# A two-layer state-space network on one core: carried states copied by VectorE, one state's B no longer spread on the scan's path, dt's bias inside its product, the first convolution shared by four engines

## The chip, the cores and the metric

The kernel runs on one core of a Trainium2 chip. A core has TensorE (PE in the profile), VectorE (DVE), ScalarE (ACT), GpSimd (POOL) and SyncE (SP, which here only issues transfers). The metric is the device time of the whole program in microseconds.

## The reference

Eight images of 48 x 48 pixels with 192 channels go through two layers. Each layer is `x + layer(group_norm(x))`.

Layer 0 is a 2D selective scan. It projects to 384 inner channels and a gate, convolves 3 x 3 by channel, and runs the scan in four directions (rows, columns, and both backwards) with 16 states per channel:

```
x_dbl = einsum('bkdl,kcd->bkcl', xs, x_proj_w)     # 12 rows for dt, 16 for B, 16 for C
dt = softplus(einsum('bkrl,kdr->bkdl', dts, dt_w) + dt_bias)
h = exp(dt * A) * h + (dt * u) * B                 # per position, channel and state
y = sum over states of h * C
ys = ys + D * xs
```

The four directions are summed, normalised over channels, gated with `silu(z)` and projected back to 192 channels.

Layer 1 runs two passes (along columns of the image, then along rows), each a sum of a forward and a backward scan over lines of 48 positions, with a convolution of three taps, the same scan with its own weights, a gate and a projection.

## The kernel before

Channels lie on the 128 partitions, three groups (`NJ`) for the 384 channels. A chunk is 8 lines of 48 positions (`T` = 384), six chunks (`NC`) to an image. An **item** is one chunk of one direction of one image: 192 items in layer 0, 192 in layer 1. An item has 48 **segments**, one for each state and channel group (`NSEG` = 16 x 3).

For one segment:

- ACT makes the decay `exp(dt * A)` (`decays`, L435).
- The input of the scan, `dt * u * B`, is made in three ways. For most states, ACT or POOL **weighs** the transposed product `dtu` by B (`weighs`, L464 on ACT in three instructions per state, L459 on POOL in one), and PE transposes it back into PSUM (`places`, L512). For the **diagonal** states (4 and 11 in layer 0) ACT or POOL makes a diagonal matrix of B (`matrices`, L483 and L480), and PE multiplies `dtu` by it (L503). For the **direct** state (8 in both layers) PE spreads B over the partitions, and DVE multiplies that by `du` ahead of the scan (`scans`, L523).
- DVE runs the scan along 384 positions (L1059 in layer 0, L1298 in layer 1).
- After the three segments of a state, POOL multiplies the three results by C in place (`gathers`, L548), and PE transposes and sums them over the states into `y` (`adds`, L565). Four `h` buffers are in flight.

In layer 0 a direction's scan runs on from chunk to chunk, so the last state of an item is kept in `carry` and is the first value of the next item's scan. `put_carry` copies the last column of `h` (three values per partition) before the product with C; it is on POOL (L1030), at 16 copies for each of 160 items.

Each pair of items is prepared by `project`: PE multiplies `u` by `x_proj` (`xd_ps`, L295), an evacuation puts the 44 rows into `xd`, SP sends the C rows to memory so that they can be fetched spread over the partitions (`cc`), PE makes dt from the first 12 rows (`dt_ps`, L344), and ACT or DVE evacuates it with the bias (`biased`, L229 and L231). A softplus follows on ACT, then `products`: POOL makes `du = dt * u` (L372), PE transposes it, and ACT or DVE copies it to `dtu`.

The order of everything is made by a planner (`Plan`). Each piece of work is a `Need` with a due time counted in segments, a cost for each engine that could do it, and what must be done before it. The planner gives each to the engine that could start it first, and of several ready ones it takes the one due first. So a changed cost or due time moves instructions between engines and along their queues. `late` puts off the due time of a piece for one engine.

The rest of layer 0 is laid between the segments: `prologues` (projection and convolution of the next image, on PE by diagonal matrices, L767), `enters` (projections of items and their table loads), `tails` (norm, gate and projection of a finished chunk, run in the last six items of each image). The first image has no scan to hide behind; `first` does its projection and convolution. There PE convolves channel group 0 and four chunks of group 2, and DVE the rest (`by_vector`, L839 and L841).

Of the kernel before, what the change touches and what calls it, by code (L numbers as in the profile page):

```python
# [35 lines left out]

DIRECT = ((8,), (8,))

# [144 lines left out]
class Common:  # L183


    def __init__(self, ctx, tc):
# [23 lines left out]
        )  # L210

    def tables(self):

        self.nc.scalar.preload_act_table_set("natural_log_exp_and_others")
# [61 lines left out]
    def project(self, plan, pool, p, pair, lo, mid, hi):  # L276

        nc, mark = self.nc, plan.mark
        tiles = {}
        dts, evacs = [], []
        for i, item in enumerate(pair):
            g, wts = 2 * p + i, item["wts"]
            turned = item.get("turned")
            across = (lambda v: v.rearrange("p (h w) -> p h w", w=RT)) if turned else rows
            at = pace(mid if i else lo, hi if i else mid, 12)
            for j in range(NJ):  # L290
                n = Need(at(), {PE: item["cost"][0]}, item["ready"] if j == 0 else (), bank=(j == 0))
                yield n
                if j == 0:
                    ps, k = self.bank(n, "xd_ps"), n.bank
                nc.tensor.matmul(  # L295
                    across(ps[:E, :T]), wts["xp"][:, j, :], item["u"](j),
                    start=(j == 0), stop=(j == NJ - 1),
                )
            xd = pool.tile([E, T], F32, tag="xd", name="xd", bufs=1)
            got = Need(at(), COPY, [n] + self.xd_used, frees=k)  # L300
            yield got
            if turned:
                self.copy(
                    got.e, xd.rearrange("p (w h) -> p w h", h=S),
                    ps[:E, :T].rearrange("p (h w) -> p w h", w=RT),
                )
            else:
                self.copy(got.e, xd, ps[:E, :T])

            def send(e, i=i, xd=xd):  # L310
                if i == 0:
                    tiles["bc"] = self.bcd.tile([2, N, T], F32, tag="bc", name="bc")
                nc.sync.dma_start(tiles["bc"][i], xd[R + N : E, :])
                pair[i]["bc"] = tiles["bc"][i]

            after = [got] + ([mark("cc", g - 5, N // 2 - 1)] if g >= 6 else [])
            sent = Need(at(), {SP: 0.1}, after, lag=DMA, sets=[mark("bc", g)])
            yield sent
            send(SP)
            n = Need(at(), {PE: 0.3}, [got], bank=True)  # L320
            yield n
            ps, k = self.bank(n, "bt_ps"), n.bank
            for b in range(TB):
                nc.tensor.transpose(
                    ps[:, b * E : (b + 1) * E], xd[:, b * P : (b + 1) * P], self.ident[:E, :E]
                )
            after = [n] + ([mark("place", (g - 2 - i) * NSEG - 1)] if g >= 4 else [])
            n = Need(at(), {ACT: 0.16, DVE: 0.19}, after, frees=k, sets=[mark("bt", g)])
            yield n
            if i == 0:  # L330
                bt = pool.tile([P, 2, TB, E], F32, tag="bt", name="bt", bufs=2)
            item["bt"] = bt[:, i]
            self.copy(n.e, bt[:, i].rearrange("p b e -> p (b e)"), ps[:, : TB * E])
            for j in range(NJ):
                after = [got]
                if j == 0 and g >= 3:
                    after.append(mark("exp", (g - 2) * NSEG - 1))
                n = Need(at(), {PE: 0.83}, after, bank=True)
                yield n
                ps = self.bank(n, "dt_ps")  # L340
                if j == 0:
                    dt = pool.tile([P, NJ, T], F32, tag="dt", name="dt", bufs=3)
                    dts.append(dt)
                nc.tensor.matmul(  # L344
                    ps[:, :T], wts["dtw"][:, j * P : (j + 1) * P], xd[:R, :], start=True, stop=True
                )
                evacs.append(plan.then(
                    Need(at(), BIAS, [n], frees=n.bank),
                    lambda e, dt=dt, j=j, ps=ps, wts=wts: self.biased(
                        e, dt[:, j, :], ps[:, :T], wts["dtb"][:, j : j + 1]  # L350
                    ),
                ))
            self.xd_used = [n, sent]
        for item, dt in zip(pair, dts):
            item["dt"] = dt
        return evacs
# [4 lines left out]

    def products(self, plan, pool, items, others, diagonal):

        nc, mark = self.nc, plan.mark
        last = max(n for n in range(N) if n not in others)
        for g, item in enumerate(items):
            after = [mark("dt", g)] + ([mark("multiplied", g - 2), mark("turned", g - 2)] if g >= 2 else [])
            n = Need(g * NSEG - 20 - item.get("sooner", 0), {POOL: item["cost"][1]}, after, sets=[mark("du", g)])
# [32 lines left out]
    def stream(self, plan, pool, items, direct, diagonal, decay, scan, finish, held, kept, weighed):  # L401
# [66 lines left out]
        def matrices():  # L468
            for i, item in enumerate(items):
                for n in sorted(diagonal):  # L470
                    after = [mark("bt", i)]
                    if placed:
                        after += [mark("place", placed[-1] + j) for j in range(NJ)]
                    need = Need(i * NSEG + NJ * n - 6, {POOL: 0.8, ACT: 0.72}, after, sets=[mark("matrix", i, n)])
                    yield need
# [59 lines left out]
        def gathers():  # L535

            for f in range(total // NJ):
# [3 lines left out]
                if "carry" in item:  # L541
                    need = Need(NJ * f + 2.5, {POOL: 0.15}, after, sets=[mark("carry", i, n)])
                    yield need
                    item["carry"](need.e, n, hs[f])
# [60 lines left out]
        for lane in (fetches, decays, weighs, matrices, places, scans, gathers, adds):  # L605
            plan.start(lane())
        plan.start(self.products(plan, pool, items, (*direct, *diagonal), diagonal))


@with_exitstack  # L610
def layer0(ctx, cm, x, xs, x2, w, norm):
# [12 lines left out]

    cw, cb, xp, dtw, dtb = [load(n) for n in ("conv_w", "conv_b", "xp", "dtw", "dtb")]
    A, D, lnw, lnb, wout = [load(n) for n in ("A", "D", "ln_w", "ln_b", "out")]
# [18 lines left out]
    per = 4 * NC  # L645
    span = per * NSEG

    def piece(b, c, due, tag="xc", bufs=2, after=(), of=x):
# [156 lines left out]
    def first():  # L805
# [22 lines left out]
        def by_vector():  # L828

            for c in range(NC):  # L830
                for j in (1, 2) if c < 2 else (1,):
                    to = rows(u[:, j, c * T : (c + 1) * T])
                    for t in range(9):
# [6 lines left out]
                        else:  # L840
                            nc.vector.scalar_tensor_tensor(to, of, cw[:, j, t : t + 1], to, ALU.mult, ALU.add)  # L841

        plan.start(by_vector())

        def by_tensor(j, chunks, made):
# [13 lines left out]
        n = yield from by_tensor(0, range(2, NC), made)  # L859
        made = yield from matrices(2, -60, [n])  # L860
        n = yield from by_tensor(2, range(2, NC), made)
        yield Need(0, {SP: 0.1}, [mark("conv", j, c) for j in range(NJ) for c in range(NC)], sets=[mark("free")])
# [4 lines left out]
    def enters():  # L867
# [5 lines left out]
        for p in range(last + 1):  # L873
# [3 lines left out]
            if q < 3 and p < last:  # L877
                lo, mid, hi = g * NSEG - 56, g * NSEG - 46, g * NSEG - 30
                if q == 0 and b:
                    n = Need(lo - 10, {SP: 0.3}, [mark("du", g - 1), mark("v", b)], lag=9.0)  # L880
# [146 lines left out]
    def put_carry(e, q, h, rev):  # L1027
        to, of = carry[:, q * NJ : (q + 1) * NJ], h[:, :, 0 if rev else T - 1]
        if e == POOL:
            nc.gpsimd.tensor_copy(to, of)  # L1030
        else:
            nc.scalar.copy(to, of)

    items = []
    for b in range(NIMG):
        for k in range(4):
            rev = k >= 2
            order = range(NC - 1, -1, -1) if rev else range(NC)
            for n, c in enumerate(order):
                item = dict(  # L1040
                    b=b, k=k, c=c, reverse=rev, carried=(n > 0), A=A[:, k],
                    wts=dict(xp=xp[:, k], dtw=dtw[:, k, :], dtb=dtb[:, k, :]),
                    u=lambda j, k=k, c=c: by_rows(seen(u, j, k, c), k), turned=k % 2,
# [46 lines left out]
def layer1(ctx, cm, x2, xw, dst, w, norm):  # L1090
# [25 lines left out]

    cb, cw, dtb, A, D, wout = [load(n) for n in ("conv_b", "conv_w", "dtb", "A", "D", "out")]
    cm.negative_exp(A)
# [133 lines left out]
    def begins():  # L1252


        for p in range(pairs):
# [8 lines left out]
            for d in range(2):  # L1264
                i = 2 * p + d
                items[i].update(
                    D=D[:, 2 * stage + d], A=A[:, 2 * stage + d], ready=[mark("silu", i)] + loaded,
                    wts=dict(xp=xp[:, d], dtw=dtw[:, d], dtb=dtb[:, 2 * stage + d]),
                )
# [104 lines left out]
def laid_out(a):  # L1374
# [7 lines left out]
    def model(v):  # L1382

        v = v.reshape(*v.shape[:-2], NM, CP, v.shape[-1])
        return np.moveaxis(v, -2, 0)

    t = {}
    t["x"] = a["x"].reshape(NIMG, L, NM, CP).transpose(0, 3, 2, 1)
# [6 lines left out]
    t["w0_xp"] = np.moveaxis(inner(g("x_proj_w")), 2, 3)  # L1395
    t["w0_dtw"] = g("dt_w").transpose(2, 0, 1)
    t["w0_dtb"] = inner(g("dt_bias"))
    t["w0_A"] = np.moveaxis(inner(g("A_logs").reshape(4, DI, N).transpose(0, 2, 1)), 2, 3)
# [8 lines left out]
    t["w1_xp"] = np.moveaxis(inner(g("x_proj_w")), 2, 3)  # L1407
    t["w1_dtw"] = g("dt_proj_w").transpose(2, 0, 1)
    t["w1_dtb"] = inner(g("dt_proj_b"))
    t["w1_A"] = np.moveaxis(inner(g("A_log").transpose(0, 2, 1)), 2, 3)  # L1410
# [24 lines left out]
```

## Time and profile before

| | |
|---|---|
| median of 3 runs | 21024.0 us (21023.82 to 21025.34) |
| profiled execution | 21021.07 us, its span 21019.3 us |
| PE busy | 20233.5 us (96%) |
| DVE busy | 19835.8 us (94%) |
| ACT busy | 20092.6 us (96%) |
| POOL busy | 19933.6 us (95%) |
| layer 0's last POOL product begins | about 10515 us |
| granted TensorE clock | 0.996 |

A group's row names line, engine, operation, the tile written and those read, shapes and count; then busy time, mean duration in ns, and the idle time of the engine just before these instructions with what ended it. Where an engine overlaps instructions, busy time over count is less than the mean duration. A row of the timeline gives start, length, engine, line, operation and count of a run of equal instructions.

### The profile page before, as it was taken

To read this page: it belongs to the slowest core of one execution; us is meant where nothing else is said; L and a number is where in the kernel's file an instruction comes from. 1 tells how busy PE (TensorE), PEld (TensorE's weight loads), DVE (VectorE), ACT (ScalarE), POOL (GpSimd) and SP (SyncE) were. 2 spreads that over 40 slices of the span, in tenths; PEclk is the share of its full clock that TensorE was granted. 3 is DMA by queue.
4 is the path that set the end of the run, shared out by engine and by line. 5 is a ranking of instruction groups with operands and counts; after the bars stand their busy time and mean duration, and the time that the engine had idled before them with its cause. 6 is when DMAs were issued, how large, how long until landed. Compare 5 with 4: busy or idle time off the path is not lost.

```text
span 21019.3 us, 391720 instructions
## 1 busy us (share of the span) xinstructions
PE 20233.5 (96%) x138640; PEld 15731.1 (75%) x138640; DVE 19835.8 (94%) x25014; ACT 20092.6 (96%) x38482; POOL 19933.6 (95%) x10537
## 2 busy tenths in 40 slices
PE   9999999999999999998899999999999999999999
PEld 6777777777777777777767777777777777777777
DVE  7999999999999999999989999999999999999999
ACT  7999999999999999999989999999999999999999
POOL 7999999999999999999989999999999999999999
PEclk9999999999999999999999999999999999999999
DMA  2222222222222222222222222222222222222222
GB/s 78 76 87 72 87 72 76 87 73 85 75 76 88 72 87 75 74 79 64 71 61 65 65 65 65 65 65 65 66 67 67 68 67 68 68 68 67 68 69 66
DMA packets 728906, 1512.36 MB, mean 72 GB/s; under 512 B 181508, under 2 KB 324484, under 8 KB 726824
## 3 DMA queue, kind: packets, MB, share of 16 engines
q1 hardware_dynamic: 724768, 1485.21, 22.8%
q8 instruction: 1106, 18.12, 0.4%
q14 instruction: 848, 6.95, 0.1%
q10 hardware_dynamic: 2184, 2.08, 0.0%
HBM read 1382.03 MB, written 104.99 MB: 71 GB/s over the span
## 4 chain that ended last, share of the span: by engine, by line
PE 57%; DVE 17%; ACT 10%; POOL 9%; issue 6%; DMA 1%; DVEq 0%; POOLq 0%; SPq 0%; ACTq 0%
PE y L565 18%; PE b L512 17%; DVE h L1298 9%; POOL h L548 7%; PE dt_ps L344 4%; ACT bT L464 3%; DVE h L1059 3%; PE xd_ps L295 3%; PE cv_ps L767 3%; PE b L503 2%; PE o_ps L1333 2%; ACT l_da L435 2%; ACT a L435 2%; PE xi_ps L1190 2%; PE z_ps L1240 2%
## 5 line engine op out<-in xcount | busy, mean ns | idle before, releaser
L548 POOL TENSOR_TENSOR h<-h,cc 128x1152 f32<-128x1152 f32 x6144 | 16177.2, 2647 | 719.3 <-DVE h L1298 257.5
L1298 DVE TENSOR_TENSOR_SCAN h<-l_da,b 128x384 f32<-128x384 f32 x9216 | 8110.6, 934 | 234.3 <-PE b L512 160.0
L565 PE MATMUL y<-ident,h 128*128 128x128 f32 x55296 | 7673.2, 275 | 188.9 <-POOL h L548 175.3
L512 PE MATMUL b<-ident,bT 128*128 128x128 f32 x48384 | 7402.7, 276 | 339.2 <-DVE h L1059 162.9
L1059 DVE TENSOR_TENSOR_SCAN h<-a,carry,b 128x384 f32<-128x384 f32 x7680 | 7201.6, 994 | 413.5 <-PE b L512 215.5
L464 ACT ACTIVATE bT<-dtu,bt 128x384 f32<-128x384 f32 x13026 | 7518.3, 606 | 54.9 <-PE b L512 45.5
L565 PEld LDWEIGHTS y<-ident,h 128*128 128x128 f32 x55296 | 6273.8, 141 | 1621.5 <-POOL h L548 708.2
L512 PEld LDWEIGHTS b<-ident,bT 128*128 128x128 f32 x48384 | 5557.4, 141 | 2022.0 <-issue 629.0
L435 ACT ACTIVATE a<-dt,l_A 128x384 f32<-128x384 f32 x9216 | 5282.5, 607 | 166.3 <-DVE h L1059 152.8
L435 ACT ACTIVATE l_da<-dt,l_A 128x376 f32<-128x376 f32 x9216 | 5107.6, 600 | 36.0 <-DVE h L1298 33.8
L459 POOL TENSOR_TENSOR bT<-dtu,bt 128x1152 f32<-128x1152 f32 x1034 | 2188.4, 2118 | 43.8 <-PE b L512 34.0
L1059 DVE TENSOR_TENSOR_SCAN h<-a,b 128x384 f32<-128x384 f32 x1536 | 1357.3, 936 | 131.3 <-PE b L512 73.2
L372 POOL TENSOR_TENSOR du<-dt,u 128x1152 f32<-128x1152 f32 x384 | 1072.2, 2792 | 148.6 <-ACT dt L360 139.8
L344 PE MATMUL dt_ps<-xd,l_dtw 12*128 12x384 f32 x2304 | 1039.6, 533 | 11.9 <-DVE dt L231 3.2
L295 PE MATMUL xd_ps<-u,l_xp 128*44 128x384 f32 x2304 | 959.2, 505 | 21.9 <-DVE z L1305 13.9
L767 PE MATMUL cv_ps<-pad,diag 128*128 128x384 f32 x2376 | 951.2, 488 | 0.0
L1240 PE MATMUL z_ps<-xt,l_z 96*128 96x384 f32 x2304 | 919.9, 490 | 16.5 <-DVE u L1215 11.2
L503 PE MATMUL b<-db,dtu 128*128 128x128 f32 x6912 | 925.1, 279 | 10.0 <-DVE h L1059 9.3
L1333 PE MATMUL o_ps<-z,l_out 128*96 128x384 f32 x2304 | 921.0, 488 | 5.7 <-DVE z L1305 5.0
L503 PEld LDWEIGHTS b<-db,dtu 128*128 128x128 f32 x6912 | 850.7, 193 | 83.7 <-DVE h L1059 42.4
L1190 PE MATMUL xi_ps<-xt,l_u 96*128 96x384 f32 x2304 | 894.8, 499 | 14.0 <-DMA l_z<-in_w_in 6.4
L1215 DVE SCALAR_TENSOR_TENSOR u<-xi_ps,l_conv_w,u 128x376 f32<-128x376 f32 (+1 forms) x1152 | 683.4, 593 | 43.4 <-ACT u L1209 22.2
(125 smaller groups left out, 14638.7 us busy)
## 6 DMA issues: line engine op xcount, KB each, us to landing
cc<-bc SPq DMA_DIRECT2D x3072, 384.0 KB, 3.5
xc<-in_x SPq DMA_DIRECT2D x186, 288.0 KB, 4.3
z<-v SPq DMA_DIRECT2D x144, 192.0 KB, 2.0
z<-z SPq DMA_DIRECT2D x48, 576.0 KB, 6.1
v<-v SPq DMA_DIRECT2D x126, 192.0 KB, 1.9
u<-v SPq DMA_DIRECT2D x21, 1152.0 KB, 9.1
xc<-in_xs SPq DMA_DIRECT2D x48, 288.0 KB, 4.2
x<-xc SPq DMA_DIRECT2D x48, 288.0 KB, 3.0
```

What stands on the lines that cost most here:

```text
L295: nc.tensor.matmul(across(ps[:E, :T]), wts["xp"][:, j, :], item["u"](j), start=(j == 0), stop=(j == NJ - 1),)
L344: nc.tensor.matmul(ps[:, :T], wts["dtw"][:, j * P : (j + 1) * P], xd[:R, :], start=True, stop=True)
L435: nc.scalar.activation(dst, src, AF.Exp, scale=item["A"][:, j, n : n + 1])
L459: nc.gpsimd.tensor_tensor(to, of, by.to_broadcast((P, TB, DI)), ALU.mult)
L464: nc.scalar.activation(to[:, b, :], of[:, b, :], AF.Copy, scale=by[:, b, :])
L503: nc.tensor.matmul(ps[:, b * P : (b + 1) * P], item["dtu"][:, b, j * P : (j + 1) * P], dbs[i, n][:, b, :], start=True, stop=True,)
L512: nc.tensor.transpose(ps[:, b * P : (b + 1) * P], of, self.ident)
L548: nc.gpsimd.tensor_tensor(h, h, c, ALU.mult)
L565: nc.tensor.matmul(item["sum"][b][:, j * P : (j + 1) * P], hs[f][:, j, b * P : (b + 1) * P], self.ident, is_transpose=True, skip_group_che ...
L767: nc.tensor.matmul(rows(ps[:, :T]), diag[:, t, :], of[:, c * RT + t // 3 : (c + 1) * RT + t // 3, t % 3 : t % 3 + S], start=(t == 0), stop ...
L1059: nc.vector.tensor_tensor_scan(order(h[:, at % NJ, :]), order(a), order(b[:, :T]), carry[:, at : at + 1] if item["carried"] else 0.0, ALU. ...
L1298: nc.vector.tensor_tensor_scan(h[:, at % NJ, :], a, b[:, :T], 0.0, ALU.mult, ALU.add)
```

## The change

- `put_carry` runs on DVE, as a maximum over an axis of one element.
- Layer 0 has no direct state: state 8 is weighed like the others. `products` no longer waits for the direct state's multiplications where there are none.
- `xd` becomes one constant tile of 45 rows, set to 1.0 at the start; its last row stays 1.0. The weights of dt get 45 rows: the 12 of before, 32 of zeros and the bias. The product then holds the bias, and its evacuation is a plain copy. `dtb` is not loaded.
- The planner's costs for the diagonal matrices change, and ACT takes them later.
- In the first image's convolution, channel group 2 from chunk 1 on is done by ACT (one tap) and POOL (the sum); PE keeps group 0, DVE group 1 and the first chunk of group 2.
- The first item's steps are due 60 segments earlier (`SOON`).
- The four directions are taken in the order 0, 1, 3, 2, so that the tails, which work on chunks of rows, go with direction 2, whose chunks are chunks of rows.

```diff
-DIRECT = ((8,), (8,))
+DIRECT = ((), (8,))
...
+        self.xd = self.const.tile([E + 1, T], F32, name="xd")
+        nc.gpsimd.memset(self.xd, 1.0)
...
-            xd = pool.tile([E, T], F32, tag="xd", name="xd", bufs=1)
+            xd = self.xd
...
-                self.copy(got.e, xd, ps[:E, :T])
+                self.copy(got.e, xd[:E], ps[:E, :T])
...
-                    ps[:, :T], wts["dtw"][:, j * P : (j + 1) * P], xd[:R, :], start=True, stop=True
+                    ps[:, :T], wts["dtw"][:, j * P : (j + 1) * P], xd, start=True, stop=True
                 )
                 evacs.append(plan.then(
-                    Need(at(), BIAS, [n], frees=n.bank),
-                    lambda e, dt=dt, j=j, ps=ps, wts=wts: self.biased(
-                        e, dt[:, j, :], ps[:, :T], wts["dtb"][:, j : j + 1]
-                    ),
+                    Need(at(), COPY, [n], frees=n.bank),
+                    lambda e, dt=dt, j=j, ps=ps: self.copy(e, dt[:, j, :], ps[:, :T]),
...
-            after = [mark("dt", g)] + ([mark("multiplied", g - 2), mark("turned", g - 2)] if g >= 2 else [])
+            after = [mark("dt", g)] + ([mark("turned", g - 2), *[mark("multiplied", g - 2)] * direct] if g >= 2 else [])
...
-                    need = Need(i * NSEG + NJ * n - 6, {POOL: 0.8, ACT: 0.72}, after, sets=[mark("matrix", i, n)])
+                    need = Need(i * NSEG + NJ * n - 6, {POOL: 0.78, ACT: 0.88}, after, sets=[mark("matrix", i, n)], late={ACT: LATE})
...
-                    need = Need(NJ * f + 2.5, {POOL: 0.15}, after, sets=[mark("carry", i, n)])
+                    need = Need(NJ * f + 2.5, {DVE: 0.1}, after, sets=[mark("carry", i, n)])
...
+    SOON = 60
...
-                for j in (1, 2) if c < 2 else (1,):
+                for j in (1, 2) if c == 0 else (1,):
...
+        def by_two():
+
+            j, added = 2, []
+            for c in range(1, NC):
+                to = rows(u[:, j, c * T : (c + 1) * T])
+                for t in range(9):
+                    of = pads[j][:, c * RT + t // 3 : (c + 1) * RT + t // 3, t % 3 : t % 3 + S]
+                    near = [mark("pad", j, a) for a in range(c - 1, min(c + 2, NC))] if t == 0 else ()
+                    n = Need(first_due(c), {ACT: 0.52}, [*near, *added[-2:-1]])
+                    yield n
+                    if t == 0:
+                        nc.scalar.activation(
+                            to, of, AF.Identity, scale=cw[:, j, 0:1], bias=cb[:, j : j + 1]
+                        )
+                        continue
+                    sq = pool.tile([P, T], F32, tag="sq", name="sq", bufs=2)
+                    nc.scalar.activation(rows(sq), of, AF.Copy, scale=cw[:, j, t : t + 1])
+                    added.append(plan.then(
+                        Need(first_due(c), {POOL: 0.87}, [n], sets=[mark("conv", j, c)] if t == 8 else ()),
+                        lambda e, to=to, sq=sq: nc.gpsimd.tensor_tensor(to, to, rows(sq), ALU.add),
+                    ))
+
         plan.start(by_vector())
+        plan.start(by_two())
...
-        made = yield from matrices(2, -60, [n])
-        n = yield from by_tensor(2, range(2, NC), made)
...
+                if p == 0:
+                    lo, mid, hi = lo - SOON, mid - SOON, hi - SOON
...
-        if e == POOL:
+        if e == DVE:
+            nc.vector.tensor_reduce(to, of.unsqueeze(2), mybir.AxisListType.X, ALU.max)
+        else:
             nc.gpsimd.tensor_copy(to, of)
-        else:
-            nc.scalar.copy(to, of)
...
-        for k in range(4):
+
+        for k in (0, 1, 3, 2):
...
+                    sooner=0 if items else SOON,
...
+    def as_xd(v, bias):
+
+        return np.concatenate([v, np.zeros((E - R, *v.shape[1:]), v.dtype), bias.reshape(1, *v.shape[1:])])
...
-    t["w0_dtw"] = g("dt_w").transpose(2, 0, 1)
-    t["w0_dtb"] = inner(g("dt_bias"))
+    t["w0_dtw"] = as_xd(g("dt_w").transpose(2, 0, 1), g("dt_bias"))
```

Layer 1's weights change in the same way.

## The prediction, made before the changed kernel was run

> **What bounds the kernel now.** I read the stages first, then the groups of instructions inside the first layer, then the timeline of GpSimd (POOL) and VectorE (DVE). The two stretches away from the ends show layer 0 and layer 1 in steady work:
>
> ```profile
> 500.00:10400.00 9900.00, 9440.52 (x66519) 7490.65 (x66518) 9250.25 (x11024) 9496.18 (x18540) 9509.34 (x6243) 0.99 0.25 78
> 11000.00:20800.00 9800.00, 9587.34 (x64555) 7344.21 (x64553) 9481.57 (x12544) 9501.22 (x17887) 9368.05 (x3720) 1.00 0.22 67
> ```
>
> The columns are PE, weight load, DVE, ACT, POOL. In layer 0 DVE is at 93.4%, ACT 95.9%, POOL 96.1%; in layer 1 DVE 96.8%, ACT 97.0%, POOL 95.6%. PE's figure is pipelined latency (three transposes of 275 ns take 0.49 us together), so I do not take PE for the bound. POOL in layer 0 is fuller than its busy share says:
>
> ```profile
> 2521.24 0.19 POOL L1030 COPY carry<-h 128x3 f32<-128x3 f32 x1
> 2521.51 2.65 POOL L548 TENSOR_TENSOR h<-h,cc 128x1152 f32<-128x1152 f32 x1
> 2524.10 0.19 POOL L1030 COPY carry<-h 128x3 f32<-128x3 f32 x1
> ...
> 10464.40 7.86 POOL L548 TENSOR_TENSOR h<-h,cc 128x1152 f32<-128x1152 f32 x3
> ```
>
> One carry and one product take 2524.10 - 2521.24 = 2.86 us; three products with no carry take 7.86, so 2.59 to 2.62 each. A carry costs 0.27 us of POOL's queue, not 0.19. The 0.08 us beside each is entered as idle: 2451 x 0.08 = about 175 us. POOL's real load in the window is 9509 + 175 = 9684 of 9900, 97.8%. POOL bounds layer 0, ACT is close behind, DVE has the room. The groups that the change touches, in that window:
>
> ```profile
> L459 POOL TENSOR_TENSOR bT<-dtu,bt 128x1152 f32<-128x1152 f32 x333 | 705.3, 2118 | 8.5 <-PE b L512 7.1 <-PE y L565 1.4
> L1030 POOL COPY carry<-h 128x3 f32<-128x3 f32 x2451 | 467.1, 191 | 103.0 <-DVE h L1059 91.5 <-PE b L512 5.7 <-PE xi_ps L716 2.8
> L480 POOL TENSOR_TENSOR db<-ident,bt 128x384 f32<-128x384 f32 x31 | 25.9, 835 | 1.3 <-PE b L503 1.3
> L523 DVE TENSOR_TENSOR b<-b,du 128x384 f32<-128x384 f32 x549 | 297.8, 543 | 4.2 <-PE b L512 3.7
> L464 ACT ACTIVATE bT<-dtu,bt 128x384 f32<-128x384 f32 x6144 | 3570.1, 606 | 16.5 <-PE b L512 12.6 <-PE y L565 0.4
> L483 ACT ACTIVATE db<-ident,bt 128x128 f32<-128x128 f32 x1005 | 327.1, 391 | 4.9 <-PE b L503 4.6
> L222 ACT COPY dtu<-du_ps 128x384 f32<-128x384 f32 x506 | 234.1, 471 | 30.6 <-PE du_ps L379 26.8
> L229 ACT ACTIVATE dt<-dt_ps,l_dtb 128x384 f32<-128x384 f32 x363 | 209.3, 577 | 42.4 <-PE dt_ps L344 36.9 <-ACT a L435 0.2
> ```
>
> **The change part by part.** Counts are from the instruction lists of the two builds, durations from the rows above (busy over count where an engine overlaps its instructions).
>
> POOL, layer 0: 2560 carries leave, -2560 x 0.27 = -691. State 8 is now weighed like the others, and 96 of these fall to POOL: +96 x 2.12 = +203. The planner's new prices move diagonal matrices to it, 35 -> 210: +175 x 0.83 = +145. The first convolution brings 40 adds, priced by `acc<-acc,z` of the same size at 1.01 us: +40. Nine fewer `diag` products: -3. Sum -306.
>
> ACT, layer 0: weighing 6432 -> 6720, +288 x 0.58 = +167; matrices 1047 -> 522, -525 x 0.325 = -171; dt by copy instead of bias, 384 x 0.577 -> 362 x 0.47 = -51; the small evacuations shift by about -13; 45 convolution taps at 0.5 to 0.6, +25. Sum -43.
>
> DVE, layer 0: 576 multiplications by du leave, -576 x 0.543 = -313. Evacuations and nine fewer convolution taps: about -5. 2560 reductions of one element come. No row of before shows that operation. Nearest are short operations with one input outside POOL's way:
>
> ```profile
> 1410.99 2.53 DVE L258 TENSOR_TENSOR gn_d<-gn_d 96x2 f32<-96x2 f32 x1
> 1413.56 0.16 DVE L259 TENSOR_TENSOR gn_d<-gn_d,gn_mv 96x2 f32<-96x2 f32 x1
> 1413.64 1.01 DVE L1059 TENSOR_TENSOR_SCAN h<-a,carry,b 128x384 f32<-128x384 f32 x1
> 1414.57 0.13 DVE L265 TENSOR_SCALAR gn<-gn_ps 96x2 f32<-96x2 f32 x1
> 1414.62 1.90 DVE L1059 TENSOR_TENSOR_SCAN h<-a,carry,b 128x384 f32<-128x384 f32 x2
> ```
>
> At 1414.57 a short operation lets the next scan start 0.05 us later. One that needs the instruction before it pays that one's full end first: a scan starts its successor after 0.91 but ends after 1.00. In the new list 1907 of the 2560 reductions stand directly behind the scan they need: 0.09 + 0.03 + 0.05 = 0.17 each; the other 653 cost 0.05 to 0.08. Mean 0.145 us, sum +371. Bounds: 0.05 (+128) and 0.25 (+640). The Trainium skill speaks against a reduction here: "VectorE: DVE Perf Modes", Rules for kernel authors, calls it the slowest DVE operation on a hot path. That rule is about long rows; the same page's errata table (58 cycles plus one per element) gives an estimate of 64 ns for three elements. By that the sum would be +163, by the nearest rows +371; I take the rows. DVE nets +53.
>
> In the window (a factor 0.955 of the layer) the loads become POOL 9684 - 292 = 9392, ACT 9496 - 41 = 9455, DVE 9250 + 51 = 9301. ACT is then fullest and the three are as even as in layer 1, where the fullest runs at 97.0%. 9455 / 0.97 = 9748, so -152, for the layer -159. Bounds: if the fullest reaches POOL's 97.8%, 9668, -243 for the layer; if the mean share of the three stays (9477 before, 9383 after), -98.
>
> The new wait: a product on POOL overwrites h and must now let DVE's reduction read it first. Behind it stand POOL's next products and the y transposes of PE. In 305 cases one or two scans of the next state, and in 348 some other instruction, stand ahead of the reduction. POOL now waits for a scan at 107 carries and 35 products of 2931, so most of the delay falls where POOL is behind anyway; if all 142 paid 0.2 to 1 us it would be 30 to 140, and that is in the range.
>
> Edits at nothing: 45 rows instead of 12 in the dt product (12 rows take 533 ns, 128 rows take 505 in the `xd_ps` product); the ACT queue issues two `dtb` loads fewer and a taller `dtw`, in the first 4 us, while the norm waits for `xc`; SP issues 4339 transfers in both. State 8's transposes read bT instead of a spread bt: 276 ns in both forms. Direction 3 ahead of direction 2 moves the tails beside unturned items; DVE is idle 6 us in all before `acc` adds, so neither a gain nor a loss of size lies there. If that cover went, it would be some us for each of 8 images.
>
> Layer 1 has only the dt copies and what the planner reshuffles: ACT -16 (293 x 0.577 -> 278 x 0.47, 39 more weighings, small shifts), DVE -10, POOL 13 weighings fewer, -27. A mean of 18; I take -15, with plus or minus 20 for the reshuffled order.
>
> The start. PE is full from 60 to 240 us, and the first scan stands behind it:
>
> ```profile
> 97.33 5.22 POOL L372 TENSOR_TENSOR du<-dt,u 128x1152 f32<-128x1152 f32 x2 [85.40 <-ACT dt L360]
> ...
> 109.00 4.32 DVE L1059 TENSOR_TENSOR_SCAN h<-a,b 128x384 f32<-128x384 f32 x5
> ```
>
> PE loses 36 products of two passes of 0.327 us, 24 us, and the first two projections are no longer threaded through them (they spread over 72 to 94 us; without the convolutions between them about 13 us). Alone that is -10 to -15 at the first scan and as much after it. Against it: DVE's taps read two SBUF tensors, and POOL was idle until 97 us. The row 1410.99 shows such an operation stretched from 0.16 to 2.53 us while POOL runs a product. The Trainium skill, "SBUF — State Buffer", Who interferes with whom, says the same as an exclusive lock. DVE has some 50 taps of 0.64 us left when POOL begins its first 24 adds: 32 + 24 us, plus 9 us of du and bT, all before the first scan, reach from 49 to about 114 us if nothing overlaps, to 95 if everything does. By the trace's PE alone -25; with the lock 0 to +5. I take -8, range -25 to +10.
>
> Sum: -159 - 15 - 8 = -182 against the profiled execution's 21021.1 (span 21019.3), which is 2.9 below the median of 21024.0. That is 20842 for the median.
>
> **The rivals.**
> Evener still (0.17): the planner priced the carry at 0.15 on POOL where it took 0.27, so other engines ran into POOL's lag. With that gone the fullest engine reaches 97.8%, and with the start's full -25 the time is about 20740, at most -350, 20675.
> DVE becomes the bound (0.14): at 0.23 per reduction DVE has 9250 + 0.955 x (589 - 318) = 9509; at its 96.8% of layer 1 that is 9823, -80 for the layer, 20920 in all. For it: three quarters of the reductions are dependent. Against: 0.17 covers that.
> The reduction waits for POOL (0.06): should it take POOL's SBUF access as the gn_d products do, each could wait up to 2.6 us. The break-even is 0.265 us per reduction; a third of them waiting 1.3 us gives 0.58, DVE 10364 / 0.968 = 10707, some +845, 21850. Against: reciprocals with one SBUF input stay at 0.13 to 0.16 in all 16 cases, and the SBUF page says a reduction never contends on this chip; no run yet shows it.
> Nothing moves (0.04): gains eaten by the gather's new wait.
>
> **How the numbers follow.** The case worked out has 0.59 and spans 20750 to 20910; with the rivals the range is 20670 to 20965. It leaves out the lock and the tails. A difference of 0.2% (42 us) is about what a measurement can tell. Faster 0.90, same 0.04, slower 0.06.
>
> **What would show it.** POOL's products at 2.6 us apart with no carry between; the reduction group on DVE with a mean duration near 0.15 us, and DVE's idle time halved; the layer change some 160 us earlier; the first scan between 95 and 114 us; layer 1 within 35 us of its length. A reduction above 0.26 us per piece, or POOL idle behind reductions, would make it wrong.

## The result, and the profile after

The changed kernel takes 20885.2 us (median of 4 runs, 20883.4 to 20891.4) against 21024.5 for the kernel before: a ratio of 0.9934, interval 0.9917 to 0.9951. That is 139 us less where 182 were forecast, inside the range. The profiled execution has a span of 20882.9 us. Of all runs below, one execution of e6 took 33099 us at a granted clock of 0.65 and is left out.

First where the time left. The beginning of layer 1's first product on POOL, in the timeline of each (before, then changed), splits the span:

```profile
10612.14 2.63 POOL L548 TENSOR_TENSOR h<-h,cc 128x1152 f32<-128x1152 f32 x1
```

```profile
10495.70 2.63 POOL L550 TENSOR_TENSOR h<-h,cc 128x1152 f32<-128x1152 f32 x1
```

| | layer 1's first product | from there to the end |
|---|---|---|
| before | 10612.1 us | 10407.2 us |
| changed | 10495.7 us | 10387.2 us |

Layer 0 gave 116 us, layer 1 gave 20. The start gave nothing that lasts: the first scan came at 106.0 instead of 109.0 us and item 4 (counted from 0) began 17 us earlier, but item 6 began 2 us later.

The busy times of the two steady stretches (columns PE, weight load, DVE, ACT, POOL), in the changed kernel:

```profile
500.00:10300.00 9800.00, 9419.57 (x66600) 7523.08 (x66599) 9312.27 (x12984) 9440.25 (x18300) 9433.25 (x4058) 0.99 0.26 78
10900.00:20700.00 9800.00, 9593.93 (x64704) 7360.72 (x64703) 9499.33 (x12582) 9512.50 (x17959) 9358.70 (x3713) 1.00 0.22 67
```

The first window holds 2936 products against 2932 in the longer one of before, so the loads can be compared directly. DVE, ACT and POOL stand at 9312, 9440 and 9433 us, where 9301, 9455 and 9392 were forecast. As shares that is 95.0, 96.3 and 96.3%. The loads came out as worked; ACT's share did not reach the 97.0% that the forecast took.

The groups that answer to the carried states, first POOL's products before (in the window of the prediction, 500 to 10400), then the changed kernel's first window:

```profile
L548 POOL TENSOR_TENSOR h<-h,cc 128x1152 f32<-128x1152 f32 x2932 | 7746.1, 2647 | 273.7 <-DVE h L1059 52.3 <-issue 14.6 <-POOL h L548 6.2
```

```profile
L550 POOL TENSOR_TENSOR h<-h,cc 128x1152 f32<-128x1152 f32 x2936 | 7712.8, 2654 | 357.8 <-DVE carry L1056 177.3 <-PE b L514 56.8 <-issue 29.9
L1056 DVE TENSOR_REDUCE carry<-h 128x3 f32<-128x3 f32 x2456 | 376.4, 153 | 62.0
```

POOL's products now wait for DVE's reduction: 177 of 358 us of idle time. Before, products and carries together were idle 377 us, but 196 of that was the 0.08 us beside each of the 2451 copies, so real waiting has grown from about 180 to 358 us. How a reduction sits in DVE's queue, and what POOL does at that moment:

```profile
2511.67 0.16 DVE L1056 TENSOR_REDUCE carry<-h 128x3 f32<-128x3 f32 x1
2511.78 2.82 DVE L1087 TENSOR_TENSOR_SCAN h<-a,carry,b 128x384 f32<-128x384 f32 x3
2514.64 0.16 DVE L1056 TENSOR_REDUCE carry<-h 128x3 f32<-128x3 f32 x1
2514.72 1.01 DVE L1087 TENSOR_TENSOR_SCAN h<-a,carry,b 128x384 f32<-128x384 f32 x1
```

```profile
2505.70 2.66 POOL L550 TENSOR_TENSOR h<-h,cc 128x1152 f32<-128x1152 f32 x1 [0.35 <-DVE carry L1056]
2509.05 2.66 POOL L550 TENSOR_TENSOR h<-h,cc 128x1152 f32<-128x1152 f32 x1 [0.69 <-DVE carry L1056]
...
2513.73 5.25 POOL L550 TENSOR_TENSOR h<-h,cc 128x1152 f32<-128x1152 f32 x2
```

Three scans and their reduction take 2514.72 - 2511.78 = 2.94 us, where three scans alone take 3 x 0.91 = 2.73: 0.21 for a dependent reduction here. Of that 0.08 is the reduction's own start to start, the rest the wait for the scan's end. Over the whole run one carried scan starts 0.92 us after another, and 1.10 us with a reduction between them (medians, the second of 1654 cases), so 0.18 is usual. POOL runs products 2.6 us apart with nothing between, as forecast.

At the start, the list of DVE's taps of the first convolution (minimum, median and maximum in ns), changed and before, and the stretch ahead of the first scan in the changed kernel:

```profile
L844 DVE SCALAR_TENSOR_TENSOR u<-acc,l_conv_w,u x56: 608/619/2873, 40.4 to 118.8; 128x384 f32<-128x384 f32 x56
```

```profile
L841 DVE SCALAR_TENSOR_TENSOR u<-acc,l_conv_w,u x64: 606/619/621, 41.0 to 92.1; 128x384 f32<-128x384 f32 x64
```

```profile
89.62 8.96 DVE L844 SCALAR_TENSOR_TENSOR u<-acc,l_conv_w,u 128x384 f32<-128x384 f32 x7
...
100.20 1.01 DVE L228 COPY dtu<-du_ps 128x384 f32<-128x384 f32 x2
```

```profile
101.35 2.35 POOL L461 TENSOR_TENSOR bT<-dtu,bt 128x1152 f32<-128x1152 f32 x1 [6.46 <-DVE dtu L228]
```

Before, no tap took over 0.621 us; now one takes 2.873, and seven take 8.96 us while POOL makes `du` (two products from 89.36 to 94.90). POOL's adds in the convolution are held up as well: they take 1.19 us beside taps and 1.00 otherwise. The copies to `dtu` stand in DVE's queue behind those taps, and POOL's first weighing waits 6.46 us for them.

### The profile page after: what moved, and what is told of

It is laid out like the page before. It is cut to its first block, busy times and chain, and to the rows that moved or that the text cites. A ratio compares the mean times of both kernels' runs of the same rounds, so it can differ in the third digit from the quotient of the medians.

```text
span 20882.9 us, 392004 instructions
## 1 busy us (share of the span) xinstructions
PE 20165.0 (97%) x138568; PEld 15742.8 (75%) x138568; DVE 19899.3 (95%) x27055; ACT 20031.8 (96%) x38259; POOL 19854.2 (95%) x8267
## 5 line engine op out<-in xcount | busy, mean ns | idle before, releaser
L514 PE MATMUL b<-ident,bT 128*128 128x128 f32 x50112 | 7716.7, 276 | 321.3 <-DVE h L1087 133.2
L466 ACT ACTIVATE bT<-dtu,bt 128x384 f32<-128x384 f32 x13353 | 7701.8, 607 | 47.9 <-PE b L514 36.6
L1087 DVE TENSOR_TENSOR_SCAN h<-a,carry,b 128x384 f32<-128x384 f32 x7680 | 7289.2, 997 | 273.1 <-PE b L514 167.4
L514 PEld LDWEIGHTS b<-ident,bT 128*128 128x128 f32 x50112 | 5770.4, 141 | 2110.7 <-issue 607.7
L461 POOL TENSOR_TENSOR bT<-dtu,bt 128x1152 f32<-128x1152 f32 x1117 | 2365.9, 2119 | 55.8 <-PE b L514 21.8
L348 PE MATMUL dt_ps<-xd,l_dtw 45*128 45x384 f32 x2304 | 1042.9, 535 | 7.3 <-ACT bt L226 3.0
```

The lines of the kernel that those rows point to most:

```text
L348: nc.tensor.matmul(ps[:, :T], wts["dtw"][:, j * P : (j + 1) * P], xd, start=True, stop=True)
L461: nc.gpsimd.tensor_tensor(to, of, by.to_broadcast((P, TB, DI)), ALU.mult)
L466: nc.scalar.activation(to[:, b, :], of[:, b, :], AF.Copy, scale=by[:, b, :])
L514: nc.tensor.transpose(ps[:, b * P : (b + 1) * P], of, self.ident)
L1087: nc.vector.tensor_tensor_scan(order(h[:, at % NJ, :]), order(a), order(b[:, :T]), carry[:, at : at + 1] if item["carried"] else 0.0, ALU. ...
```

## The experiments

All start from the changed kernel. The kernel before ran beside each set and gave medians from 21011.6 to 21017.6; the changed kernel, run again on one of the chips (e9), gave 20881.0. Differences below are between ratios, times 21020.

The intervals set e1, e2 and e5 apart from the changed kernel. Those of e3, e7, e8 and e11 overlap with its own, so a difference of 20 to 30 us between ratios is not shown by them. For these the traces help. Layer 1 takes 10387.2 to 10392.3 us in the changed kernel and in every run but e3, and layer 0 ends between 10482.8 and 10500.4 us in the changed kernel and in e4, e6, e9, e10 and e12, which do the same work in other orders. I take a shift of layer 0's end beyond this spread as real.

**e1, the carried states back on POOL.**

```diff
-                    need = Need(NJ * f + 2.5, {DVE: 0.1}, after, sets=[mark("carry", i, n)])
+                    need = Need(NJ * f + 2.5, {POOL: 0.15}, after, sets=[mark("carry", i, n)])
```

> The changed kernel with the carried states copied by POOL again (planner's price 0.15), everything else as changed. Theory A (the gain is load taken off POOL): 2560 copies at 0.27 us, 691 us of POOL, come back while state 8 stays weighed, so POOL is fuller than in the kernel before although the planner can push weighings and matrices to ACT; DVE loses about 410 us. The three engines' loads rise by 280 in sum, 93 each: 20980 to 21150 us, with DVE idle for over 900 us of layer 0. Rival B (the gain comes from the other edits, the carry only changes places): within 40 us of the changed kernel's 20885.

20970.6 us, ratio 0.9979 (0.9970 to 0.9988): 95 us slower than the changed kernel. The window of layer 0:

```profile
500.00:10300.00 9800.00, 9344.97 (x66058) 7447.52 (x66057) 8929.50 (x10458) 9473.67 (x18426) 9538.86 (x6351) 1.00 0.24 78
```

DVE is idle for 870 us, and POOL is at 9539 plus 0.08 beside each of some 2400 copies, about 9730 of 9800. Theory A holds, though the time lies 9 us under its range. The loss is in layer 0 (its end at 10574.9 instead of 10495.7, the rest 10388.3).

**e2, state 8 direct again.**

```diff
-DIRECT = ((), (8,))
+DIRECT = ((8,), (8,))
```

> The changed kernel with state 8 direct again in layer 0 (DVE multiplies the spread B by du), carried states still on DVE. Theory A (three engines balanced, DVE has no room for both): DVE gets 313 us more, about 9610 in a window of 9800 where it had 9312; at the 96 to 97% that an engine reaches here that is 9910 to 10010, so +110 to +220: 20990 to 21100 us. Rival B (ACT bounds layer 0, and 192 weighings fewer help it): 20780 to 20860.

21001.9 us, ratio 0.9996 (0.9987 to 1.0004): 130 us slower.

```profile
500.00:10300.00 9800.00, 9378.43 (x65890) 7414.67 (x65889) 9465.15 (x13349) 9306.20 (x17936) 9192.70 (x3893) 1.00 0.24 78
```

Here DVE is the fullest of the three (96.6%), with ACT and POOL emptier. So the two main edits are one exchange: the copies leave POOL, and DVE can only take them because it gives up the multiplications. With either one undone most of the gain is gone.

**e3, dt's bias in the evacuation again.**

```diff
-                    ps[:, :T], wts["dtw"][:, j * P : (j + 1) * P], xd, start=True, stop=True
+                    ps[:, :T], wts["dtw"][:R, j * P : (j + 1) * P], xd[:R, :], start=True, stop=True
...
-                    Need(at(), COPY, [n], frees=n.bank),
-                    lambda e, dt=dt, j=j, ps=ps: self.copy(e, dt[:, j, :], ps[:, :T]),
+                    Need(at(), BIAS, [n], frees=n.bank),
+                    lambda e, dt=dt, j=j, ps=ps, wts=wts: self.biased(
+                        e, dt[:, j, :], ps[:, :T], wts["dtb"][:, j : j + 1]
+                    ),
...
```

> The changed kernel with dt's bias added in the evacuation again (12 rows in the product), both layers. Theory A: the biased evacuation costs 0.10 us more on ACT (640 of them) and 0.06 to 0.1 more on DVE (512), some 100 us of load over three engines and two layers, so +30 to +45: 20915 to 20930, half of it in layer 1. Rival B (hidden, only the order is reshuffled): within 15 us of 20885. Rival C (ACT bounds alone): +65.

20907.0 us, ratio 0.9948 (0.9933 to 0.9963): 29 us slower, just under theory A. But it is not half and half. Layer 1 begins at 10494.8 us, as in the changed kernel, and from there to the end it takes 10413.1 against 10387.2: the whole difference, and the whole gain of layer 1, is this edit. In layer 0 it brings nothing that shows. ACT's evacuations of dt over both layers, here and in the changed kernel:

```profile
L233 ACT ACTIVATE dt<-dt_ps,l_dtb 128x384 f32<-128x384 f32 x626 | 359.5, 574 | 60.1 <-PE dt_ps L348 49.8 <-POOL bT L463 0.2
```

```profile
L226 ACT COPY dt<-dt_ps 128x384 f32<-128x384 f32 x640 | 303.4, 474 | 67.2 <-PE dt_ps L348 55.6
```

**e4, the first image's convolution and `SOON` as before.** The short form of the edit:

```diff
-                for j in (1, 2) if c == 0 else (1,):
+                for j in (1, 2) if c < 2 else (1,):
...
-        plan.start(by_two())
...
+        made = yield from matrices(2, -60, [n])
+        n = yield from by_tensor(2, range(2, NC), made)
...
-    SOON = 60
+    SOON = 0
...
```

> The changed kernel with the first image's convolution as before (four chunks of group 2 on PE, none on ACT and POOL, chunk 1 of it on DVE) and SOON at 0. Theory A (the start gained nothing by the end of the first image because DVE's taps and POOL's adds hold each other up): the first scan returns to 109 us, items 1 to 4 are 10 to 17 us later than in the changed kernel, and the whole is within 10 us of 20885. Rival B (PE's relief at the start is worth its 24 us): 20905 to 20915.

20876.2 us, ratio 0.9934 (0.9919 to 0.9949): no difference. Item 4 lost its 17 us and was 3 behind the kernel before, and by item 6 this run and the changed kernel were level. In the details the expectation missed: the first scan came at 103.1, where 109 was expected, and items 1 to 4 were 2 to 21 us later than in the changed kernel, not 10 to 17. The start is worth nothing by the end of the first image.

**e5, a plain copy on DVE in place of the maximum.**

```diff
-            nc.vector.tensor_reduce(to, of.unsqueeze(2), mybir.AxisListType.X, ALU.max)
+            nc.vector.tensor_copy(to, of)
```

> The changed kernel with the carried states copied on DVE by a plain copy instead of the maximum of one element; nothing else differs. Theory A (a plain copy of floats within SBUF takes the port pair that POOL's products hold, as the Trainium skill's page SBUF — State Buffer says and as the gn_d products show; a reduction does not): each of 2560 copies waits for up to one product of 2.6 us, mean 0.5 to 1.3, so DVE becomes the bound: 22000 to 24000 us, the copy's mean duration 0.6 to 1.5 us. Rival B (three elements are too short to matter, or this pattern does not take the pair): duration 0.15 us and within 20 us of the changed kernel's ratio of 0.993.

21722.9 us, ratio 1.0339 (1.0318 to 1.0359): 851 us slower than the changed kernel, 712 slower than the one before. The copies in the window of layer 0:

```profile
L1056 DVE COPY carry<-h 128x3 f32<-128x3 f32 x2256 | 1224.2, 543 | 57.2
```

Three values take 543 ns in the mean, 171 in the median and up to 3241, against 153 for the maximum of the same three values. The mechanism is theory A's. A copy that waits ends with POOL's instruction, and one that starts with POOL idle does not wait; DVE, then POOL:

```profile
3002.59 0.17 DVE L1056 COPY carry<-h 128x3 f32<-128x3 f32 x1
...
3019.33 1.13 DVE L1056 COPY carry<-h 128x3 f32<-128x3 f32 x1
```

```profile
2999.60 2.64 POOL L550 TENSOR_TENSOR h<-h,cc 128x1152 f32<-128x1152 f32 x1 [0.26 <-PE b L514]
...
3018.32 2.12 POOL L461 TENSOR_TENSOR bT<-dtu,bt 128x1152 f32<-128x1152 f32 x1
```

In the whole trace 1140 of the 2560 copies take over 0.2 us. Each of them began while POOL was at work, and in the median it ended 0.03 us after POOL's instruction did. Of the 854 that began with more than 0.3 us of POOL's instruction left, 849 waited. So fewer than half wait because the others find POOL idle or nearly done, and both the mean and the time (277 us) lie under the ranges that were expected. This is the prediction's third rival, on an operation that the change avoids.

**e6, the reduction one scan later.**

```diff
-                    need = Need(NJ * f + 2.5, {DVE: 0.1}, after, sets=[mark("carry", i, n)])
+                    need = Need(NJ * f + 3.5, {DVE: 0.1}, after + [mark("scan", NJ * f + 3)], sets=[mark("carry", i, n)])
```

> The changed kernel with each reduction put behind the first scan of the next state instead of directly behind the scan that it needs. It no longer stalls DVE for the end of that scan (0.116 us at some 1900 of 2560: 220 us of DVE's load leave), but POOL's product waits 0.9 us longer wherever POOL stands ready. Theory W (POOL's wait for the reduction, 177 us in the window, is what took part of the gain back): the wait grows to 300 to 450 us, and the time by 20 to 100 us over the changed kernel (ratio 0.9945 to 0.998). Rival D (DVE's load bounds): 50 to 100 us faster than the changed kernel (0.9885 to 0.991).

20876.4 us, ratio 0.9935 (0.9918 to 0.9951): no difference. DVE's busy time fell from 9312 to 9147 us and POOL's wait for the reduction from 177 to 147 us. Rival D is refuted: DVE's load is not what bounds. Theory W expected POOL's wait to grow, which it did not, so what the wait is worth stays untested here.

**e7, the reduction reads a constant.** The carried states are left out; a reduction of zeros stands where each stood.

```diff
+    still = wp.tile([P, NJ], F32, name="still")
+    nc.gpsimd.memset(still, 0.0)
...
-            nc.vector.tensor_reduce(to, of.unsqueeze(2), mybir.AxisListType.X, ALU.max)
+            nc.vector.tensor_reduce(to, still.unsqueeze(2), mybir.AxisListType.X, ALU.max)
```

> The changed kernel with each reduction reading a small tile of zeros instead of h: the states carried from chunk to chunk are left out, the instruction count and order are the same. The reduction waits for no scan and no product waits for it. Theory W (the new wait costs): POOL's idle time falls by 150 to 180 us, DVE's load by 220, and the time by 60 to 150 us (ratio 0.986 to 0.9905). Rival S (POOL's idle time is only slack behind another bound): within 25 us of the changed kernel.

20852.9 us, ratio 0.9925 (0.9909 to 0.9942): 19 us faster by the ratio; in the trace layer 0 ends 46 us earlier, at 10449.6. POOL's products without the dependence:

```profile
L550 POOL TENSOR_TENSOR h<-h,cc 128x1152 f32<-128x1152 f32 x2950 | 7737.7, 2647 | 317.3 <-DVE h L1089 108.7 <-POOL h L550 55.8 <-issue 55.7
```

The idle time falls by 41 us only, where 150 to 180 were expected; most of what waited for the reduction now waits for the scan itself. The new wait is worth 19 to 46 us, under the 60 to 150 that theory W asked. Rival S is nearer.

The run does less than its expectation says. A reduction still writes `carry`, which the scan directly before it reads, and it still waits for that scan: between two carried scans it costs 0.18 us of DVE's queue as before. Only in the first item of a direction, whose scans read no carried value, it falls from 0.20 to 0.05 us. So DVE's busy time stayed (9309 us) where a fall of 220 was expected, and e7 tests POOL's wait alone.

**e8, the directions in the order 0, 1, 2, 3.**

```diff
-        for k in (0, 1, 3, 2):
+        for k in range(4):
```

> The changed kernel with the directions taken in the order 0, 1, 2, 3 as before, so that the tails run beside the turned items again and, as in the kernel before, on chunks of which later items still add. Theory A (no work changes, and DVE hardly waits at the sums): within 12 us of the changed kernel (ratio 0.9929 to 0.994). Rival B (the sums of a turned item cross all rows and wait for the tail's last reads of them, some us at each of 42 chunks): 30 to 100 us slower, with DVE waiting before acc.

20842.1 us, ratio 0.9920 (0.9905 to 0.9934): 29 us faster by the ratio; in the trace layer 0 ends 42 us earlier, at 10453.3 against 10495.7. Neither theory had that sign. The window:

```profile
500.00:10300.00 9800.00, 9449.17 (x66887) 7551.31 (x66885) 9339.68 (x13036) 9493.68 (x18435) 9465.47 (x4063) 0.99 0.25 79
```

ACT is at 96.9% with the same work. An image takes 1281.9 us (mean of images 1 to 6, from first scan to first scan), against 1286.6 to 1289.3 in the changed kernel and in e4, e6, e9, e10 and e12, which all end an image with direction 2. Against the changed kernel the time is gained where images meet: the first three items take 170.5 us against 174.9, and the last three 174.9 against 178.4. How a seam divides shifts by reshuffling alone (e4, with the changed kernel's order of directions, has 170.7 and 181.5), so this says where the time went and not why.

**e9, the changed kernel again; e10, the carry at its real price.** The edit of e10:

```diff
-                    need = Need(NJ * f + 2.5, {DVE: 0.1}, after, sets=[mark("carry", i, n)])
+                    need = Need(NJ * f + 2.5, {DVE: 0.17}, after, sets=[mark("carry", i, n)])
```

> The changed kernel once more, on the same chip as the next two, as the measure for their small differences. All theories: ratio 0.9925 to 0.9945.

> The changed kernel with the planner's price of a carried state at 0.17 instead of 0.10 (the mean that the trace shows is 0.16 to 0.17 of DVE's queue); no work is added or taken. Theory N (differences of some 30 us, as between the orders of the directions, come from how the planner's order happens to fall at the image ends): within 30 us of the changed kernel, of either sign, with the difference gathered at the first and last three items of an image. Rival P (the wrong price is what keeps the engines from filling): 40 to 80 us faster.

20881.0 us, ratio 0.9935 (0.9922 to 0.9947), and 20890.7, ratio 0.9939 (0.9927 to 0.9951). The price is not what keeps the engines from filling: rival P is refuted. The difference of 8 to 10 us is one example of what a reshuffled order does by itself.

**e11, three diagonal states.**

```diff
-DIAGONAL = ((4, 11), ())
+DIAGONAL = ((2, 7, 12), ())
```

> The changed kernel with three diagonal states (2, 7, 12) instead of two (4, 11) in layer 0: 192 weighings (1.5 us of ACT or 2.07 of POOL each) become matrices (0.88 or 0.78), so 150 to 190 us leave ACT and POOL together, and PE gets 1728 products in place of transposes, 0.34 us more for each of 576 segments, 196 us. Theory A (ACT and POOL bound layer 0, PE has room): the loads fall by about 80 on each, the time by 40 to 80 us against the changed kernel. Rival E (PE at 96% is the bound, or the single matrix buffer makes new waits): 50 to 200 us slower.

20914.7 us, ratio 0.9949 (0.9936 to 0.9963): 29 us slower by the ratio, 34 by the medians of e9 and e11, which ran on the same chip, and layer 0 ends at 10530.9.

```profile
500.00:10300.00 9800.00, 9517.29 (x68045) 7684.56 (x68043) 9268.49 (x12900) 9391.41 (x18340) 9319.92 (x4020) 0.99 0.26 78
```

The window holds 2926 products instead of 2936. For equal products POOL has some 80 us less than in the changed kernel, ACT only 17 less, PE 130 more, and the kernel is slower. PE is at 97.1%. Rival E had the sign, and a smaller size than it asked. Its second half, waits around the one matrix buffer, does not show: ACT waits 1.9 us for that buffer, against 5.0 in the changed kernel. PE's load is what is left of it; that it bounds is not shown, since ACT was hardly relieved. It is enough to say that taking 80 us off POOL does not help when PE gets 130 more.

**e12, the column directions exchanged.**

```diff
-        for k in (0, 1, 3, 2):
+        for k in (0, 3, 1, 2):
```

> The changed kernel with the two column directions exchanged: order 0, 3, 1, 2. No instruction is added or taken, the tails still go with direction 2. Theory N (the 40 us between the orders 0, 1, 3, 2 and 0, 1, 2, 3 are how the planner's order falls): the time lies 10 to 40 us from the changed kernel's 20883, of either sign. Theory T (it is the tails beside unturned items that cost, some 5 us an image at the image ends): within 10 us of the changed kernel, and the first and the last three items of an image stay at 175 and 178 us.

20883.8 us, ratio 0.9936 (0.9922 to 0.9949): the changed kernel's time. The first and last three items of an image stay at 176.3 and 178.8 us. Theory T is borne out and N is not, but the test is a mild one: most items take the changed kernel's time to within 0.3 us, so this exchange reshuffles little. Together with the other runs that end an image with direction 2, it makes the direction that goes last the likely cost.

## Why the prediction was right, and where it was off

**Right: POOL was the fullest of layer 0's engines, by a cost that its busy time does not show.** A carry took 0.27 us of its queue, 0.19 of them busy. Taking 691 us off it while giving 348 back is what the change lives on (e1: 95 us), together with the room that DVE got (e2: 130 us). One sum of the working is off: 2451 x 0.08 is 196, not 175, so POOL stood at 9705 of 9900, 98.0%.

**Right: the loads.** Each of the three was forecast within 41 us of about 9400, POOL within 20 with the sum put right. A reduction directly behind its scan was put at 0.17 and costs 0.18 in the median.

**Off: what the loads are worth.** The term that was too large is "for the layer -159", by "the fullest runs at 97.0%" as in layer 1. ACT and POOL stopped at 96.3%: 9440 / 9800. With 97.0% the same loads would need 9732 us, so 68 us of the window are in that share. Layer 0 as a whole gave 116, the start's zero included. The prediction's lower bound, that the mean share of the three engines stays, was nearer: it was 95.8% before, with POOL at 9705, and is 95.9% now. That bound was -98 in the window, -103 for the layer.

Three causes were tried. The new wait for the reduction is 19 to 46 us of it (e7), the planner's price none (e10), the order of directions 29 to 42 (e8). The prediction also dismissed PE ("I do not take PE for the bound"). In layer 1 of the kernel before, PE's busy time was 9587 of 9800 us, 97.8%, above the three engines that were compared, and e11 shows that a lighter POOL does not help when PE gets more to do. The sum over three engines may have been one engine short; how much PE bounds stays open. The new prices of the diagonal matrices were not undone by themselves.

**Off: the wait for the reduction.** It stood at nothing in the sum and at 30 to 140 us in the range, and POOL's idle time behind reductions, which was named as a sign of being wrong, came to 177 us. Its effect on the time was smaller than that (e7). DVE's idle time was to halve and fell from 650 to 488 us in the windows.

**Off: an edit costed at nothing.** "Direction 3 ahead of direction 2" was covered by DVE's 6 us of idle time before the `acc` sums. That looked at one engine's wait at one line. e8 puts 29 to 42 us on it, which is the "some us for each of 8 images" that the prediction named for the case that the cover fails. The other reshuffles moved layer 0's end by 13 us at most. Which wait at the seams of the images is the first I did not settle.

**Right: the start.** The taps and POOL's work hold each other up, -25 to +10 was given and 0 came. The size taken, -8, was off by that. **Right: layer 1**, -15 against -20, though the reason was narrower than written: all of it is the bias (e3). The longer product costs nothing, as forecast: 535 ns with 45 rows, 533 with 12.

**Nearly right: the size of the rival with the lock.** It put 0.58 us on each operation, +845 us on layer 0 against the kernel before, and 21850 us in all. e5, with the operation that does wait, measured 0.543 us, +738 us on layer 0 and 21723 us. The parts fit less well: a third of the operations were to wait 1.3 us, and 45% took 1.0 us in the mean.

The sum, forecast and measured: layer 0 without the start -159 and about -117; the start -8 and 0; layer 1 -15 and -20.

## What to carry to other kernels

A short operation costs its engine the distance between starts around it, not its busy time: look at the timeline for the gap beside it before deciding which engine should have it. Moving work to an engine pays only with room made there, so judge such edits as a pair, and then ask all engines, TensorE too, what they are given. A reordering that changes no work can still cost or gain time: here a difference showed at the seams where images meet, and one engine's wait at one line had not announced it. Before reading a run without a dependence, look whether another one keeps the same wait.

## What the runs showed of the hardware

A copy of three floats from SBUF to SBUF on VectorE took 543 ns in the mean and up to 3241 while POOL ran products, and a maximum over one element of the same three values 153 ns and at most 165 (e5 and the changed kernel). No copy that began with POOL idle took over 0.2 us (656 of them), while 2293 of the 2560 maxima began beside a working POOL and did not wait. The Trainium skill's "SBUF — State Buffer", Who interferes with whom, says that a copy can enter a mode that takes the port pair shared with GpSimd and a reduction on this chip cannot; the numbers agree with both. Operations with two inputs in SBUF wait in the same way: taps of 0.62 us reached 2.87 beside POOL's `du`, and each of the 20 that took over 0.65 us ended 0.41 us after the POOL instruction beside it.

A reduction directly behind a scan that it depends on cost 0.18 us of DVE's queue in the median, whether it read the scan's result (the changed kernel) or overwrote the value that the scan had read (e7). With neither it cost 0.04 to 0.05 (e6, and the first items in e7). Taking that stall away at most places (e6: DVE's busy time down by 165 us) changed nothing in the time; DVE stood at 95.0%, under ACT and POOL.
